# Cross-attention and mixture-of-experts block: a re-ordered prologue, with weight turns among the first row maxima and the first V projections inside batch 0

## The chip, the cores and the metric

The kernel runs on one core of one Trainium2 chip. The metric is the device time in microseconds (us); a figure for a kernel is the median of its runs. Engines are TensorE (PE, with its weight loads as PEld), VectorE (DVE), ScalarE (ACT), GpSimd (POOL) and SyncE (SP, which here only issues DMAs).

## The reference

For 8 batches of x with 256 rows and 512 columns. The attention works on the normalised rows of x as channels, the 512 columns being tokens; the feed-forward part works on rows as tokens of width 512.

```
t = layernorm(x)                       # over the 512 columns
q, k, v = Wq@t + bq, Wk@ctx + bk, Wv@ctx + bv          # 256x256 weights
dot = einsum('bhdt,bhds->bhts', q, k) / 4              # 16 heads of 16
mask = tmask[..., :, None] * smask[..., None, :]       # all ones here
dot = mask*dot - (1 - mask)*1e6
x = x + einsum('bhts,bhds->bhdt', softmax(dot)*mask, v)
n = layernorm(x)
x = x + n + shared_ffn(n) + top2_of_8_experts(n)       # 512 -> 352 -> 512
```

All is float32 but the experts, which are bfloat16.

## The kernel before

Order is by hand: each engine runs its instructions in the order in which the program issues them, and the framework adds only the waits that data and buffers need. A buffer pool with n buffers makes the (n+1)th tile of a tag wait for the readers of the first.

Prologue (lines 117 to 196 and 953 to 989). DMAs go out on two queues: SP carries x, ctx, the transposed-mask rows `mnat` and the bias of V `bvb`; ACT carries Wq, the broadcast mask `mb`, Wk, Wv and four small DMAs of the biases of q and k (L140). The biases are turned on TensorE (L145), and 16 small VectorE operations (L148 to L161) make the columns `alpha`, `beta`, `mine`, from which `extra_rows` makes, for each head group and side, a 128x512 tile that is added to q or k and holds bias and masking rows. Wq, Wk and Wv are turned on TensorE in `turn_square` and copied to SBUF by ScalarE. VectorE takes the statistics of x (L302 to L305), GpSimd the inverse square root (L307), VectorE normalises to `xm` (L326) and multiplies it by the mask (L328), GpSimd multiplies ctx by the mask (L314).

A head group G is half of the heads that one projection makes: `project_qk(G, side)` gives q or k for G and G + 1 with two accumulated matmuls, each recorded as two, into one bank (L373), and two VectorE operations out of it (L379). There are 4 groups to a batch, 32 in all.

The softmax of a group needs row maxima first: `row_max` multiplies q by k on 32-row tiles of the array (two logical matmuls, four recorded, L390) into a two-bank tile of `ps_s`, and VectorE reduces it (L392). Eight of these make a group; `take_max` turns the maxima and subtracts them from q (L398, L399). Then `exp_scores` multiplies the other way round (L410) and ScalarE takes exp (L412); `attend` multiplies by V (L425), four 32-column tiles each.

The first loop (L982, called the head loop here) makes the ten row maxima that run ahead: all eight of G = 0 and two of G = 1. They alternate between the banks `s1` and `s2`. After every second one of the first eight, `project_v` projects a quarter of V (psv, L342; VectorE, L346); the router's weights are turned after the first; `take_max(0)` follows the eighth.

The main loop runs over batches b, groups g and steps h = 0 to 7: a step is one row maximum for the next group and one exp, with attend in every second step, and projections, the division, the residual and other work in fixed steps. `plan` is a list of further thunks per step of a batch (step n = 8g + h). In batch 0 it holds eight `clear` DMAs that write zeros to DRAM and ten turns of the shared expert's weights (`weight_thunks`: 6 `up_rows` of four transposes, 4 `down_rows` of three; each call also issues loads, up to three ahead, on SP), whose copies `evacuate` deals out to VectorE and ScalarE in turn. `load_batch(b + 1)` is called in step 6.

Buffers that matter: `ps_m` tag `mm` has two banks for all turns, projections and V; `ps_s` has one tile for `s1` and one for `s2`; `acc` (five buffers) holds the natural weights and biases before they are turned; `extra` has three; `ctx` and `mb` one each.

Of the kernel before, what the change touches and what calls it, by code (L numbers as in the profile page):

```python
# [9 lines left out]
F32 = mybir.dt.float32  # L10
# [3 lines left out]
ALU = mybir.AluOpType  # L14
# [20 lines left out]
def xattn_ffn_kernel(  # L35
# [76 lines left out]
    def load_square(W):  # L112
        nat = five.tile([P, 2, C], F32, tag="acc", name="wnat")
        nc.scalar.dma_start(out=nat, in_=W.rearrange("(o p) c -> p o c", p=P))
        return nat

    wq_nat = load_square(Wq)
    load_batch(0, (nc.sync, nc.scalar))
    wk_nat, wv_nat = load_square(Wk), load_square(Wv)


# [9 lines left out]

    bnat = five.tile([2 * NG, 4, 2, HD], F32, tag="acc", name="bnat")
    nc.vector.memset(bnat, 0.0)
    for side, bias in enumerate((bq, bk)):
        by_group = bias.rearrange("(c a j d) -> a c j d", a=2, j=4, d=HD)
        for a in range(2):
            row = NG * side + 2 * a
            nc.scalar.dma_start(out=bnat[row : row + 2, :, a, :], in_=by_group[a])  # L140
    alpha = const.tile([P, 2, 2, NG // 2], F32, name="alpha")
    beta = const.tile([P, 2, 2], F32, name="beta")
    mine = const.tile([P, 2], F32, name="mine")
    pt = ps_m.tile([P, 2, 2, NG // 2], F32, tag="mm", name="pt")
    nc.tensor.transpose(  # L145
        pt.rearrange("p s a c -> p (s a c)"), bnat.rearrange("r j a d -> r (j a d)"), ident[: 2 * NG, : 2 * NG]
    )
    nc.vector.tensor_scalar(alpha[:, 0], pt[:, 0], 0.25, None, ALU.mult)  # L148
    nc.vector.tensor_copy(alpha[:, 1], pt[:, 1])
    for a in range(2):  # L150
        r = HD * (1 - a)
        R0, R1, R2 = (rowis[:, r + i : r + i + 1] for i in range(3))
        nc.vector.tensor_reduce(mine[:, a : a + 1], rowis[:, HD * a : HD * a + HD], AX.X, ALU.add)
        nc.vector.tensor_scalar(beta[:, 0, a : a + 1], R0, -BIG, None, ALU.mult)
        nc.vector.tensor_add(beta[:, 1, a : a + 1], R0, R1)
        for R, big in ((R1, -BIG), (R0, BIG)):
            nc.vector.scalar_tensor_tensor(
                alpha[:, 0, a], R.to_broadcast([P, 2]), big, alpha[:, 0, a], ALU.mult, ALU.add
            )
        nc.vector.tensor_sub(alpha[:, 1, a], alpha[:, 1, a], R1.to_broadcast([P, 2]))  # L160
        nc.vector.tensor_add(beta[:, 1, a : a + 1], beta[:, 1, a : a + 1], R2)  # L161
    mhalf = const.tile([P, 1], F32, name="mhalf")
    nc.gpsimd.memset(mhalf, -0.5)
    rank = const.tile([P, E], F32, name="rank")
# [36 lines left out]
    ys = dram.tile([NT * P, T], F32, name="ys")  # L201
    ACC = [[dram.tile([P, T], F32, name=f"accd{b}_{tt}") for tt in range(2)] for b in range(NB)]

    WqT = wts.tile([P, 2, 2, 4, 2, HD], F32, name="WqT")
    WkT = wts.tile([P, 2, 2, 4, 2, HD], F32, name="WkT")
    WvT = wts.tile([P, 2, C], F32, name="WvT")

    def turn_square(nat):  # L210
        pt = ps_m.tile([P, 2, 2, P], F32, tag="mm", name="pt")
# [11 lines left out]
    def load_router():  # L223
        nat = five.tile([E, T], F32, tag="acc", name="wnat")
        nc.sync.dma_start(out=nat, in_=router_w)
        pt = ps_m.tile([P, NKC, E], F32, tag="mm", name="pt")
        for kc in range(NKC):
            nc.tensor.transpose(pt[:, kc, :], nat[:, kc * P : (kc + 1) * P], ident[:E, :E])
        nc.vector.tensor_copy(sguT[:, 1, :, I:], pt)

    def weight_thunks():


        def up_rows(W, dst, ic):
            i0, n = ICH[ic]
            nat = five.tile([P, T], F32, tag="acc", name="wnat")
            nc.sync.dma_start(out=nat[:n, :], in_=W[i0 : i0 + n, :])

            def go():
                pt = ps_m.tile([P, NKC, P], F32, tag="mm", name="pt")  # L240
                for kc in range(NKC):
                    nc.tensor.transpose(pt[:, kc, :n], nat[:n, kc * P : (kc + 1) * P], ident[:n, :n])
                evacuate(dst[:, :, i0 : i0 + n], pt[:, :, :n])

            return go

        def down_rows(W, dst, hc):
            nat = five.tile([P, I], F32, tag="acc", name="wnat")
            nc.sync.dma_start(out=nat, in_=W[hc * P : (hc + 1) * P, :])

            def go():
                pt = ps_m.tile([P, 3, P], F32, tag="mm", name="pt")
                for ic, (i0, n) in enumerate(ICH):
                    nc.tensor.transpose(pt[:n, ic, :], nat[:, i0 : i0 + n], ident)
                cols = slice(hc * P, (hc + 1) * P)
                evacuate(dst[:, 0:2, cols], pt[:, 0:2, :])
                evacuate(dst[: ICH[2][1], 2, cols], pt[: ICH[2][1], 2, :])
# [50 lines left out]
        return mv, rs  # L308


    def mask_context(b):
        s = S[b]
        for i in range(2):
            nc.gpsimd.tensor_mul(s["ctx"][:, i, :], s["ctx"][:, i, :], s["mb"])  # L314

    def start_stats(b, i):
        s = S[b]
# [9 lines left out]
        for i in range(2):  # L327
            engine.tensor_mul(xm[:, i, :], xm[:, i, :], s["mb"])  # L328

    def project_v(b, only=None):  # L330

        if only in (None, 0):
# [6 lines left out]
        for sc in range(4) if only is None else [only]:  # L339
# [15 lines left out]
    def extra_rows(G, side, engine):  # L355

        b, g = divmod(G, NG)
        if True:
            for a in range(2):
                t = three.tile([P, T], F32, tag="extra", name=f"extra{side}_{G + a}")  # L360
                engine.tensor_scalar(  # L361
                    t, S[b]["mb"], alpha[:, side, a, g // 2 : g // 2 + 1], beta[:, side, a : a + 1],
                    ALU.mult, ALU.add,
                )
                EXTRA[G + a, side] = t

    def project_qk(G, side):

        b, g = divmod(G, NG)
        W, rhs = ((WqT, S[b]["xm"]), (WkT, S[b]["ctx"]))[side]  # L370
# [1 line left out]
        for kc in range(2):  # L372
# [4 lines left out]
        for a in range(2):  # L377
            t = four.tile([P, T], F32, tag="qk"[side], name=f"{'qk'[side]}{G + a}")
            nc.vector.scalar_tensor_tensor(  # L379
                t, ps, mine[:, a : a + 1], EXTRA.pop((G + a, side)), ALU.mult, ALU.add  # L380
            )
            QK.setdefault(G + a, []).append(t)

    def row_max(G, tci, half, tag="s1"):

# [566 lines left out]

    for i in range(2):
        start_stats(0, i)
    extra_rows(0, 0, nc.vector)
    for nat, dst, scale in ((wq_nat, WqT, 0.25), (wk_nat, WkT, 1.0)):
        pt = turn_square(nat)
        for kc in range(2):
            for a in range(2):
                by_row = pt[:, kc, :].rearrange("p (c a j d) -> p c a j d", c=2, a=2, j=4)[:, :, a]  # L960
# [2 lines left out]
                    nc.scalar.copy(at, by_row)  # L963
                else:
                    nc.scalar.mul(at, by_row, scale)
    nc.scalar.copy(WvT, turn_square(wv_nat))
    start_norm(0, nc.vector)
    mask_context(0)


    mnat = five.tile([B * 4, P], F32, tag="acc", name="mnat")
    nc.sync.dma_start(out=mnat, in_=mask.rearrange("b o (c p) -> (b o c) p", p=P))
    mcol = const.tile([P, B * 4], F32, name="mcol")
    pt = ps_m.tile([P, B * 4], F32, tag="mm", name="pt")
    nc.tensor.transpose(pt, mnat, ident[: B * 4, : B * 4])
    nc.vector.tensor_copy(mcol, pt)
    nc.sync.dma_start(out=bvb, in_=bv.partition_broadcast(P))

    project_qk(0, 0)
    extra_rows(0, 1, nc.vector)  # L980
    project_qk(0, 1)
    for r in range(8 + LEAD):  # L982
        row_max(r // 8, r % 8 // 2, r % 2, ("s1", "s2")[r % 2])
        if r % 2 == 1 and r < 8:
            project_v(0, r // 2)
        if r == 7:
            take_max(0)
        if r == 0:
            load_router()
    weights = weight_thunks()  # L990
    casts, turns = expert_weights()
    V_AT = [(2, 5), (2, 7), (3, 1), (3, 3)]
    KEPT = 6
# [14 lines left out]
    for b in range(B):  # L1008
        plan = later + [[] for _ in range(STEPS - len(later))]
        if b == 0:  # L1010
            spread(plan, [(1.0, lambda e=e: clear(e)) for e in range(E)], [(3 * e + 8, 1) for e in range(E)])
            spread(plan, weights, [(n, 1) for n in (7, 11, 13, 15, 16, 23, 24, 27, 29, 31)])
        if 1 <= b <= 4:
            for n in range(6):
                plan[5 * n + 1].append(casts.pop(0))
# [18 lines left out]
        for g in range(NG):  # L1034
            G = NG * b + g
            for h in range(8):
# [23 lines left out]
                    start_stats(b + 1, h - 2)  # L1060
                if g == 1 and h == 5 and b + 1 < B:
                    start_norm(b + 1, nc.gpsimd)
                if (g, h) in V_AT and b + 1 < B:
                    project_v(b + 1, V_AT.index((g, h)))
                if g % 2 == 1 and h == 7 and G + 3 < last:
# [73 lines left out]
```

## Time and profile before

| | us |
|---|---|
| median of 3 runs | 918.92 |
| lowest, highest | 918.4, 925.13 |
| the profiled execution, its own time | 920.46 |
| its span in the profile | 918.7 |
| mean granted clock of TensorE | 0.987 |

Busy time of the engines in the stages that the change touches, from the view that sums busy time by stretch (length, then engine busy times with the number of instructions, the granted clock, the share of DMA and GB/s):

```profile
core 0: us, PE busy (x) PEld busy (x) DVE busy (x) ACT busy (x) POOL busy (x), PEclk, DMA share, GB/s
0.00:26.95 26.95, 10.11 (x23) 5.16 (x23) 12.88 (x37) 3.43 (x10) 10.06 (x54) 1.00 0.31 103
26.95:42.04 15.09, 13.36 (x64) 6.08 (x64) 13.96 (x21) 0.00 (x0) 1.52 (x2) 1.00 0.01 2
42.04:69.75 27.71, 24.67 (x105) 7.30 (x105) 14.27 (x15) 8.18 (x8) 3.25 (x3) 0.75 0.42 144
69.75:132.23 62.48, 55.43 (x376) 19.99 (x376) 44.97 (x68) 28.70 (x34) 17.92 (x18) 1.00 0.66 219
132.23:918.70 786.47, 745.93 (x4461) 308.34 (x4461) 508.58 (x927) 313.08 (x404) 237.18 (x247) 0.99 0.31 80
```

The rows are: the prologue up to the first row maximum; the head loop; group 0 of batch 0; groups 1 to 3; everything after. How to read it: the engine with the most busy time in a stretch is a candidate for what bounds it, but only the chain of waits says whether it was waited for. Times in the text are from the start of the span. A matmul's end is modelled, so overlapping matmuls can be listed with the same times.

### The profile page before, as it was taken

What the parts mean: (1) busy time and instruction counts of PE and PEld (TensorE: products, weight loads), DVE (VectorE), ACT (ScalarE), POOL (GpSimd) and SP (SyncE); (2) the same over time, 40 slices, a digit from 0 to 9 for tenths busy, and PEclk for the clock granted to TensorE, in tenths of its full rate; (3) what the DMA queues carried; (4) which work ended last, traced back from release to release, by engine and by line L of the source; (5) the groups of instructions that cost most, each with busy time, mean ns of one, the idle gap of its engine ahead of it and who ended that gap; (6) DMA issues with size and microseconds to landing.
All of it is one profiled execution on the core that took longest, in us unless ns stands there. A gap on an engine that the chain in (4) does not pass through costs nothing.

```text
span 918.7 us, 13426 instructions
## 1 busy us (share of the span) xinstructions
PE 849.5 (92%) x5027; PEld 346.9 (38%) x5027; DVE 594.7 (65%) x1064; ACT 353.4 (38%) x456; POOL 269.9 (29%) x324
## 2 busy tenths in 40 slices
PE   3887989999999999999999999999999899999875
PEld 1322333333333333433343334333434344445653
DVE  4847767785777677767776777677665732224477
ACT  1024444443344344434443434343434235555111
POOL 3114303532354235413450435052401110000551
PEclk9979999999999999999999999999999999999999
DMA  3049523112641353226321600020000033444785
GB/s 121 1 159 357 184 70 90 32 28 55 130 85 34 65 133 66 46 53 149 50 55 28 151 1 24 12 70 1 24 12 12 36 95 115 125 127 132 232 271 184
DMA packets 93080, 83.03 MB, mean 90 GB/s; under 512 B 58224, under 2 KB 74000, under 8 KB 92632
## 3 DMA queue, kind: packets, MB, share of 16 engines
q1 hardware_dynamic: 85360, 57.26, 21.8%
q0 software_dynamic: 4352, 19.67, 9.2%
q10 hardware_dynamic: 3304, 5.25, 1.6%
q8 instruction: 41, 0.67, 0.3%
q14 instruction: 23, 0.19, 0.1%
HBM read 41.91 MB, written 44.04 MB: 94 GB/s over the span
## 4 chain that ended last, share of the span: by engine, by line
PE 65%; DVE 16%; issue 10%; DMA 4%; POOL 3%; ACT 0%; DVEq 0%; ACTq 0%; SPq 0%; POOLq 0%
PE s L390 21%; PE av L425 9%; DVE nm L392 8%; PE psy L855 5%; PE psq L373 4%; PE pu L792 3%; PE eu L717 3%; PE eg L717 3%; PE ey L738 3%; PE psv L342 2%; PE s L410 2%; PE pgu L792 2%; PE psk L373 2%; PE pg L792 2%; DVE q L379 2%
## 5 line engine op out<-in xcount | busy, mean ns | idle before, releaser
L412 ACT ACTIVATE e<-s 128x1024 f32<-128x1024 f32 x256 | 262.0, 1023 | 431.9 <-PE s L410 431.7
L392 DVE TENSOR_REDUCE nm<-s 128x2 f32<-128x1024 f32 x256 | 312.8, 1223 | 143.1 <-PE s L410 132.4
L390 PE MATMUL s<-k,q 32*128 32x512 f32 x1024 | 289.7, 647 | 22.9 <-DVE nm L392 20.2
L410 PE MATMUL s<-q,k 32*128 32x512 f32 x1024 | 292.6, 648 | 0.0
L425 PE MATMUL av<-e,V 128*32 128x512 f32 x1024 | 137.8, 611 | 0.0
L390 PEld LDWEIGHTS s<-k,q 32*128 32x128 f32 x1024 | 77.1, 184 | 132.1 <-DVE nm L392 108.1
L307 POOL TENSOR_TENSOR rs<-ve,mhalf 128x1 f32<-128x1 f32 x32 | 18.3, 571 | 320.1 <-DVE ve L305 320.1
L361 POOL TENSOR_SCALAR extra<-mb,alpha,beta 128x512 f32<-128x512 f32 x60 | 46.2, 774 | 196.3 <-DVE q L379 195.2
L410 PEld LDWEIGHTS s<-q,k 32*128 32x128 f32 x1024 | 77.6, 185 | 3.4 <-issue 1.0
L425 PEld LDWEIGHTS av<-e,V 128*32 128x32 f32 x1024 | 20.2, 108 | 98.0 <-issue 97.9
L723 DVE SCALAR_TENSOR_TENSOR hz<-eth,eu 128x352 bf16<-128x352 f32 x35 | 18.2, 521 | 55.6 <-PE eu L717 49.4
L855 PE MATMUL psy<-sdT,h 128*128 128x512 f32 (+1 forms) x96 | 49.4, 627 | 5.0 <-DVE acc L861 3.5
L603 POOL DMA_INDIRECT xs<-xnb,at x28 | 28.0, 1002 | 70.5 <-DMA xs<-xnb,at 38.1
L373 PE MATMUL psq<-xm,WqT 128*128 128x512 f32 x64 | 35.3, 678 | 5.7 <-DVE xm L328 5.7
L766 POOL DMA_INDIRECT yg<-ys,yi x28 | 27.9, 997 | 33.6 <-DMA back<-accd 15.0
L717 PEld LDWEIGHTS <-late_ctx 128*128 128x128 bf16 x280 | 25.9, 97 | 27.5 <-issue 7.3
L792 PE MATMUL pu<-xT,sguT 128*128 128x256 f32 x128 | 35.9, 400 | 0.0
L792 PE MATMUL pg<-xT,sguT 128*128 128x256 f32 x128 | 35.0, 401 | 0.2 <-ACT logT L820 0.2
L342 PE MATMUL psv<-WvT,ctx 128*128 128x256 f32 x128 | 34.8, 394 | 0.0
L379 DVE SCALAR_TENSOR_TENSOR q<-psq,mine,extra 128x512 f32<-128x512 f32 x32 | 22.6, 746 | 17.9 <-PE psq L373 17.9
L792 PE MATMUL pgu<-xT,sguT 128*104 128x256 f32 (+1 forms) x128 | 33.8, 392 | 0.0
L743 ACT COPY ey<-ey 128x512 f32<-128x512 f32 x35 | 20.5, 586 | 32.7 <-PE ey L738 31.5
(189 smaller groups left out, 970.8 us busy)
## 6 DMA issues: line engine op xcount, KB each, us to landing
xs<-blank SPq DMA_DIRECT2D x8, 1792.0 KB
ys<-ey SPq DMA_DIRECT2D x35, 256.0 KB
x<-in_x_dram SPq DMA_DIRECT2D x8, 512.0 KB
ctx<-in_ctx_dram SPq DMA_DIRECT2D x8, 512.0 KB
back<-accd SPq DMA_DIRECT2D x14, 256.0 KB
out_dram<-back ACTq DMA_DIRECT2D x14, 256.0 KB
accd<-acc SPq DMA_DIRECT2D x12, 256.0 KB
gu<-in_L_ffn_w_gate_dram POOLq DMA_DIRECT2D x8, 352.0 KB
```

The source lines that it names most:

```text
L342: nc.tensor.matmul(ps, ct[:, kc, sc * P : (sc + 1) * P], WvT[:, kc, :], start=(kc == 0), stop=(kc == 1))
L361: engine.tensor_scalar(t, S[b]["mb"], alpha[:, side, a, g // 2 : g // 2 + 1], beta[:, side, a : a + 1], ALU.mult, ALU.add,)
L373: nc.tensor.matmul(ps, W[:, kc, g // 2].rearrange("p j a d -> p (j a d)"), rhs[:, kc, :], start=(kc == 0), stop=(kc == 1),)
L379: nc.vector.scalar_tensor_tensor(t, ps, mine[:, a : a + 1], EXTRA.pop((G + a, side)), ALU.mult, ALU.add)
L390: nc.tensor.matmul(ps[:, jj, :], q[r, tci * P : (tci + 1) * P], k[r, :], start=True, stop=True)
L392: nc.vector.reduce_max(NM[G % 2][:, tci, c0 : c0 + 33 : 32], ps, axis=AX.X)
L410: nc.tensor.matmul(ps[:, jj, :], k[r, sc * P : (sc + 1) * P], q[r, :], start=True, stop=True)
L412: nc.scalar.activation(e, ps, AF.Exp)
L425: nc.tensor.matmul(AVT[G][32 * j : 32 * j + 32, :], V[:, sc, 2 * g + j // 2, j % 2 : j % 2 + 2, :].rearrange("p o d -> p (o d)"), et[j // ...
L717: nc.tensor.matmul(ps, xT[:, kc, :], guT[:, bass.ds(e, 1), m, kc, :].rearrange("p o i -> p (o i)"), start=(kc == 0), stop=(kc == NKC - 1),)
L792: lambda kc=kc: nc.tensor.matmul(ps, gu[:, m, kc, i0 : i0 + n], xT[:, kc, :], start=(kc == 0), stop=(kc == NKC - 1))
L855: nc.tensor.matmul(t[0], get()[:n, ic, tt * P : (tt + 1) * P], d[:n, ic, :], start=(ic == 0), stop=(ic == 2))
```

## The change

- x of batch 0 is loaded first on SP, in two halves; then the four bias DMAs, now on SP, then ctx. ACT's queue keeps Wq, mask, Wk, Wv.
- The row terms (the bias transpose and the small VectorE operations) become a function, called after Wk is turned and after `xm` is made.
- The mask of ctx for batch 0 moves from GpSimd to VectorE; the four extras of groups 0 and 1 move from VectorE to ScalarE, as an activation with per-partition scale and bias.
- Wk and Wv are turned in the banks `s1` and `s2` of the scores; Wq stays in `mm`.
- k's second VectorE operation is issued after the first row maximum. The copies of `mcol` and of the router's turn go to ScalarE, and so do all copies of the shared expert's turns.
- In the head loop a turn of the shared expert's weights follows row maxima 1 to 6, 8 and 9 (eight of the ten); V is no longer projected there. Batch 0's plan keeps two turns, in steps 11 and 13.
- V of batch 0 is projected in group 0 of batch 0, in steps 0, 2, 5 and 7.

```diff
+    for i in range(2):
+        nc.sync.dma_start(out=S[0]["x"][:, i, :], in_=x[0, i * P : (i + 1) * P, :])
     wq_nat = load_square(Wq)
-    load_batch(0, (nc.sync, nc.scalar))
-    wk_nat, wv_nat = load_square(Wk), load_square(Wv)
+    nc.scalar.dma_start(out=S[0]["mb"], in_=mask[0, 0].partition_broadcast(P))
     bnat = five.tile([2 * NG, 4, 2, HD], F32, tag="acc", name="bnat")
...
-            nc.scalar.dma_start(out=bnat[row : row + 2, :, a, :], in_=by_group[a])
+            nc.sync.dma_start(out=bnat[row : row + 2, :, a, :], in_=by_group[a])
+    nc.sync.dma_start(out=S[0]["ctx"], in_=src[0].rearrange("(h p) t -> p h t", p=P))
+    wk_nat, wv_nat = load_square(Wk), load_square(Wv)
...
-                evacuate(dst[:, :, i0 : i0 + n], pt[:, :, :n])
+                nc.scalar.copy(dst[:, :, i0 : i0 + n], pt[:, :, :n])
...
+                if engine is nc.scalar:
+                    nc.scalar.activation(t, S[b]["mb"], AF.Identity, bias=be, scale=at)
...
-        for a in range(2):
+        def rows(a):
             t = four.tile([P, T], F32, tag="qk"[side], name=f"{'qk'[side]}{G + a}")
...
+        rows(0)
+        if one_now:
+            return rows
+        rows(1)
...
-    extra_rows(0, 0, nc.vector)
...
-    nc.scalar.copy(WvT, turn_square(wv_nat))
+    square(wq_nat, WqT, 0.25, ps_m, "mm")
     start_norm(0, nc.vector)
-    mask_context(0)
+    square(wk_nat, WkT, 1.0, ps_s, "s1")
+    row_terms()
+    mask_context(0, nc.vector)
+    wv = turn_square(wv_nat, ps_s, "s2")
+    extra_rows(0, 0, nc.scalar)
+    nc.scalar.copy(WvT, wv)
+    extra_rows(0, 1, nc.scalar)
+    project_qk(0, 0)
+    k_rows = project_qk(0, 1, True)
...
     for r in range(8 + LEAD):
         row_max(r // 8, r % 8 // 2, r % 2, ("s1", "s2")[r % 2])
-        if r % 2 == 1 and r < 8:
-            project_v(0, r // 2)
+        if r == 0:
+            k_rows(1)
+            pt = ps_m.tile([P, B * 4], F32, tag="mm", name="pt")
+            nc.tensor.transpose(pt, mnat, ident[: B * 4, : B * 4])
+            nc.scalar.copy(mcol, pt)
+            load_router()
+        elif r != 7:
+            weights.pop(0)[1]()
         if r == 7:
             take_max(0)
-        if r == 0:
-            load_router()
...
-            spread(plan, weights, [(n, 1) for n in (7, 11, 13, 15, 16, 23, 24, 27, 29, 31)])
+            spread(plan, weights, [(11, 1), (13, 1)])
...
+                if b == 0 and g == 0 and h in (0, 2, 5, 7):
+                    project_v(0, (0, 2, 5, 7).index(h))
```

More of the change, by code (lines that the diff above doesn't have):

```diff
@@ L115, in load_square @@
         return nat
-    wq_nat = load_square(Wq)
-    load_batch(0, (nc.sync, nc.scalar))
-    wk_nat, wv_nat = load_square(Wk), load_square(Wv)
-    ident = const.tile([P, P], F32, name="ident")
-    make_identity(nc, ident)
-    rowis = const.tile([P, 32], F32, name="rowis")
-    nc.vector.tensor_reduce(rowis, ident.rearrange("p (j r) -> p r j", j=4), AX.X, ALU.add)
+    S[0] = {
+        "x": two.tile([P, 2, T], F32, tag="x", name="x0"),
+        "mb": one.tile([P, T], F32, tag="mb", name="mb0"),
+        "ctx": one.tile([P, 2, T], F32, tag="ctx", name="ctx0"),
+    }
+    for i in range(2):
+        nc.sync.dma_start(out=S[0]["x"][:, i, :], in_=x[0, i * P : (i + 1) * P, :])
+    wq_nat = load_square(Wq)
+    nc.scalar.dma_start(out=S[0]["mb"], in_=mask[0, 0].partition_broadcast(P))
     bnat = five.tile([2 * NG, 4, 2, HD], F32, tag="acc", name="bnat")
@@ L139, in xattn_ffn_kernel @@
             row = NG * side + 2 * a
-            nc.scalar.dma_start(out=bnat[row : row + 2, :, a, :], in_=by_group[a])
+            nc.sync.dma_start(out=bnat[row : row + 2, :, a, :], in_=by_group[a])
+    nc.sync.dma_start(out=S[0]["ctx"], in_=src[0].rearrange("(h p) t -> p h t", p=P))
+    wk_nat, wv_nat = load_square(Wk), load_square(Wv)
+    ident = const.tile([P, P], F32, name="ident")
+    make_identity(nc, ident)
+    rowis = const.tile([P, 32], F32, name="rowis")
+    nc.vector.tensor_reduce(rowis, ident.rearrange("p (j r) -> p r j", j=4), AX.X, ALU.add)
     alpha = const.tile([P, 2, 2, NG // 2], F32, name="alpha")
@@ L143, in xattn_ffn_kernel @@
     mine = const.tile([P, 2], F32, name="mine")
[L144 to L149, printed above, removed]
-    for a in range(2):
[L151 to L161, printed above, removed]
     mhalf = const.tile([P, 1], F32, name="mhalf")
@@ L202, in xattn_ffn_kernel, with row_terms @@
     ACC = [[dram.tile([P, T], F32, name=f"accd{b}_{tt}") for tt in range(2)] for b in range(NB)]
+    def row_terms():
+        pt = ps_m.tile([P, 2, 2, NG // 2], F32, tag="mm", name="pt")
+        nc.tensor.transpose(
+            pt.rearrange("p s a c -> p (s a c)"), bnat.rearrange("r j a d -> r (j a d)"), ident[: 2 * NG, : 2 * NG]
+        )
+        nc.vector.tensor_scalar(alpha[:, 0], pt[:, 0], 0.25, None, ALU.mult)
+        nc.vector.tensor_copy(alpha[:, 1], pt[:, 1])
+        for a in range(2):
+            r = HD * (1 - a)
+            R0, R1, R2 = (rowis[:, r + i : r + i + 1] for i in range(3))
+            nc.vector.tensor_reduce(mine[:, a : a + 1], rowis[:, HD * a : HD * a + HD], AX.X, ALU.add)
+            nc.vector.tensor_scalar(beta[:, 0, a : a + 1], R0, -BIG, None, ALU.mult)
+            nc.vector.tensor_add(beta[:, 1, a : a + 1], R0, R1)
+            for R, big in ((R1, -BIG), (R0, BIG)):
+                nc.vector.scalar_tensor_tensor(
+                    alpha[:, 0, a], R.to_broadcast([P, 2]), big, alpha[:, 0, a], ALU.mult, ALU.add
+                )
+            nc.vector.tensor_sub(alpha[:, 1, a], alpha[:, 1, a], R1.to_broadcast([P, 2]))
+            nc.vector.tensor_add(beta[:, 1, a : a + 1], beta[:, 1, a : a + 1], R2)
     WqT = wts.tile([P, 2, 2, 4, 2, HD], F32, name="WqT")
@@ L208, in xattn_ffn_kernel, with turn_square @@
     WvT = wts.tile([P, 2, C], F32, name="WvT")
-    def turn_square(nat):
-        pt = ps_m.tile([P, 2, 2, P], F32, tag="mm", name="pt")
+    def turn_square(nat, pool, tag):
+        pt = pool.tile([P, 2, 2, P], F32, tag=tag, name="pt")
         for kc in range(2):
@@ L228, in load_router @@
             nc.tensor.transpose(pt[:, kc, :], nat[:, kc * P : (kc + 1) * P], ident[:E, :E])
-        nc.vector.tensor_copy(sguT[:, 1, :, I:], pt)
+        nc.scalar.copy(sguT[:, 1, :, I:], pt)
     def weight_thunks():
@@ L255, in go @@
                 cols = slice(hc * P, (hc + 1) * P)
-                evacuate(dst[:, 0:2, cols], pt[:, 0:2, :])
-                evacuate(dst[: ICH[2][1], 2, cols], pt[: ICH[2][1], 2, :])
+                nc.scalar.copy(dst[:, 0:2, cols], pt[:, 0:2, :])
+                nc.scalar.copy(dst[: ICH[2][1], 2, cols], pt[: ICH[2][1], 2, :])
             return go
@@ L308, in norm_stats, with mask_context @@
         return mv, rs
-    def mask_context(b):
+    def mask_context(b, engine=nc.gpsimd):
         s = S[b]
         for i in range(2):
-            nc.gpsimd.tensor_mul(s["ctx"][:, i, :], s["ctx"][:, i, :], s["mb"])
+            engine.tensor_mul(s["ctx"][:, i, :], s["ctx"][:, i, :], s["mb"])
     def start_stats(b, i):
@@ L328, in start_norm, with project_v @@
             engine.tensor_mul(xm[:, i, :], xm[:, i, :], s["mb"])
-    def project_v(b, only=None):
-        if only in (None, 0):
+    def project_v(b, only):
+        if only == 0:
             V = two.tile([P, 4, HEADS // 2, 3, HD], F32, tag="V", name=f"V{b}")
@@ L338, in project_v @@
         by_pair = lambda t: t.rearrange("p (h o d) -> p o h d", o=2, d=HD)
-        for sc in range(4) if only is None else [only]:
+        for sc in (only,):
             ps = ps_m.tile([P, C], F32, tag="mm", name="psv")
@@ L360, in extra_rows, with project_qk @@
                 t = three.tile([P, T], F32, tag="extra", name=f"extra{side}_{G + a}")
[L361 to L364, printed above, removed]
+                at, be = alpha[:, side, a, g // 2 : g // 2 + 1], beta[:, side, a : a + 1]
+                if engine is nc.scalar:
+                    nc.scalar.activation(t, S[b]["mb"], AF.Identity, bias=be, scale=at)
+                else:
+                    engine.tensor_scalar(t, S[b]["mb"], at, be, ALU.mult, ALU.add)
                 EXTRA[G + a, side] = t
-    def project_qk(G, side):
+    def project_qk(G, side, one_now=False):
         b, g = divmod(G, NG)
@@ L376, in project_qk @@
             )
-        for a in range(2):
+        def rows(a):
             t = four.tile([P, T], F32, tag="qk"[side], name=f"{'qk'[side]}{G + a}")
@@ L954, in xattn_ffn_kernel, with square @@
         start_stats(0, i)
-    extra_rows(0, 0, nc.vector)
-    for nat, dst, scale in ((wq_nat, WqT, 0.25), (wk_nat, WkT, 1.0)):
-        pt = turn_square(nat)
+    def square(nat, dst, scale, *where):
+        pt = turn_square(nat, *where)
         for kc in range(2):
@@ L973, in xattn_ffn_kernel @@
     mcol = const.tile([P, B * 4], F32, name="mcol")
-    pt = ps_m.tile([P, B * 4], F32, tag="mm", name="pt")
-    nc.tensor.transpose(pt, mnat, ident[: B * 4, : B * 4])
-    nc.vector.tensor_copy(mcol, pt)
     nc.sync.dma_start(out=bvb, in_=bv.partition_broadcast(P))
-    project_qk(0, 0)
-    extra_rows(0, 1, nc.vector)
-    project_qk(0, 1)
+    weights = weight_thunks()
     for r in range(8 + LEAD):
         row_max(r // 8, r % 8 // 2, r % 2, ("s1", "s2")[r % 2])
-        if r % 2 == 1 and r < 8:
-            project_v(0, r // 2)
+        if r == 0:
[6 more added lines that the diff above has]
+            weights.pop(0)[1]()
         if r == 7:
             take_max(0)
-        if r == 0:
-            load_router()
-    weights = weight_thunks()
     casts, turns = expert_weights()
```

## The prediction

> **What bounds the kernel now.** I read the page's chain that ended last, then the same chain in order of time for the first 50 us, then the matmul timeline for how far apart the steps of the head loop lie, then the busy time and granted clock in stretches of 3.41 us. The change touches only the prologue and batch 0, so these are the views that matter. The chain in order of time:
> ```profile
> 1.24 6.80 DMA ctx<-in_ctx_dram
> 8.06 2.00 DMA bnat<-in_L_xattn_bk_dram
> ...
> 14.96 3.79 DVE xm L326 x2
> ...
> 19.49 3.75 PE psq L373 x4
> 23.24 2.87 PE psk L373 x4
> 26.14 0.76 DVE k L379
> 26.95 1.13 PE s L390 x4
> ```
> Until 10 us everything waits for the last bias, whose DMA was issued only when ctx had landed; its transpose stands first in TensorE's queue. Then VectorE carries the chain. The two normalisations take 3.79 us, and two rows of the sources by line say why that is odd:
> ```profile
> L326 DVE TENSOR_SCALAR xm<-x,mv,rs x2: 1555/1978/2400, 14.9 to 16.3; 128x512 f32<-128x512 f32 x2
> L486 DVE TENSOR_SCALAR xn<-acc,mv,rs x1: 540/540/540, 841.6 to 841.6; 128x512 f32<-128x512 f32 x1
> ```
> The same form takes 0.54 us late in the kernel. The slow pair lies beside GpSimd's mask of ctx (L314, 14.89 to 17.55).
>
> The clock, in stretches that end where the granted clock changes:
> ```profile
> 39.06:42.48 3.42, 1.83 (x11) 0.75 (x13) 3.04 (x6) 0.00 (x0) 0.00 (x0) 1.00 0.02 5
> 42.48:45.89 3.41, 3.41 (x10) 1.01 (x8) 1.86 (x2) 0.59 (x1) 0.00 (x0) 0.50 0.00 0
> 45.89:49.30 3.41, 3.41 (x9) 1.00 (x6) 1.23 (x1) 1.23 (x2) 0.00 (x0) 0.50 0.00 0
> 49.30:52.72 3.42, 3.42 (x8) 1.19 (x10) 0.44 (x1) 0.22 (x1) 0.00 (x0) 0.50 0.00 0
> ...
> 59.54:62.96 3.42, 1.60 (x16) 0.31 (x8) 2.19 (x2) 1.66 (x2) 1.36 (x2) 1.00 0.89 304
> 62.96:66.37 3.41, 3.28 (x16) 0.71 (x16) 1.23 (x2) 1.02 (x1) 1.12 (x1) 0.50 1.08 383
> 66.37:69.78 3.41, 2.69 (x24) 1.19 (x20) 2.07 (x4) 1.02 (x1) 0.00 (x0) 1.00 1.09 386
> ```
> A stretch with little array work (39.06, 59.54) is followed by half clock, and two stretches in which TensorE was busy throughout (42.48, 45.89) did not bring the clock back, because 32-row matmuls fill a quarter of the array each. Before 42 us the view prints 1.00 for want of a record; the projections there take 0.85 us a matmul against 0.48 later, so the clock was half until about 25.4 us.
>
> **What the Trainium skill says.** (1) "TensorE: Matmul & The Clock Gate", Part 1: the clock is halved or full, decided per free-running window of about 3.4 us by how busy the array was. The trace agrees: 0.50 or 1.00, held for 3.41 us or multiples. (2) The same page, Part 4: a transpose on TensorE "doesn't count as PE-busy the same way". Half agrees: the stretch from 66.37, eight transposes among its 24, kept its clock with otherwise less work than the one from 59.54, so they count for something. (3) "SBUF — State Buffer", "SBUF: two separate sides": VectorE in a two-port mode and GpSimd lock each other out of a shared port pair. 2.40 and 1.56 us against 0.54 agree.
>
> **A measure of array work.** One unit is a 32-row matmul of 512 columns, or a 128-column transpose, a quarter of 0.48 us. A full projection matmul is 4 units, one of V 2, one of the attend's (32 columns) 1. Counted from the timeline: clock lost after 39.06 (10 units) and 59.54 (11); held after 25.41 (12.5); not regained after 18.58 (10.4) or 45.89 (9.8); regained after 49.30 (15) and 62.96 (14). So a window needs somewhere between 11 and 12.5 units to hold, 10.4 to 14 to recover.
>
> **The change part by part.**
>
> Front. x now has SP's queue to itself ahead of the biases and ctx; ACT's queue loses the four bias DMAs and carries Wq, mask, Wk, Wv. Wq landed at 5.7 us (the fourth SP DMA, bvb, was released by it then); I take x's second half at 5.5 (bounds 4.5 and 8.0, the latter ctx's landing). VectorE no longer waits for the biases: statistics 0.61 + 0.18 + 0.15 plus gaps, 6.5; GpSimd's power 0.57, 7.1; xm 0.54, 7.65; two mask products 1.27, 8.95. TensorE: Wq's turn from 5.7 (12 turns took 3.11, so 1.04 for four), Wk's, then the bias transpose. The last bias waits for Wq or x at worst (5.7), plus 2.0 of flight: 7.8 (bounds 5 and 10). Wv's turn ends about 9.2, psq starts at 9.3. The 14 small row-term operations (10.58 to 11.95, 1.4 us), then the ctx mask on VectorE (2 x 0.67), run from 8.95 to 11.7 beside psq; ctx sits behind six DMAs and lands at about 9.3. All are done before psk at 12.7, so they cost nothing; if ctx came after 11.4, psk would slip. The four extras move to ACT, idle until 45.3 us: nearest row, its 128x512 copy, 0.58 each (bounds 0.5 to 1.0), hidden by psq. Wk and Wv in the scores' banks remove the 0.33 and 0.42 us waits for a bank, counted in the turns. psq and psk took 6.62; with the clock coming back anywhere in a window I take 6.1, so psk ends 15.4, k's first STT 0.76, first row maxima T = 16.2 (bounds 14.5 and 18.5). Before: 26.95. **-10.75.**
>
> Head loop. Before, it ran from 26.95 to 42.04, 15.1 us, VectorE-bound (10 x 1.23 plus V's 4 x 0.6), with two row maxima often overlapping on different rows of the array. Now a turn stands between each two, so none overlap, and TensorE is the bound: 1.08 + 0.59 = 1.67 us a step at full clock (V's STTs gone, VectorE needs 1.23). One wait is new: k's second STT is queued on VectorE behind the first row maximum, and the router's transposes need psk's bank, which that STT frees; the second row maximum stands behind them. TensorE has 1.07 us of work, then waits until T + 3.1, and restarts at T + 3.5. If those transposes got the other bank this would be 1.4 us less (the low bound); nothing in the trace settles it, and I take the wait. At full clock: six steps with turns (two of them smaller) about 10, the eighth with its maximum and take_max 2.6, two more with turns of three 3.2: 19.3 us.
>
> At half clock a row maximum takes 1.69 (42.04) and a turn about 0.95 (0.75 the smaller ones): 3.5 + 6 x 2.65 + 3.2 + 2 x 2.45 = 27.5 us.
>
> Which? Around T, from psk's end to T + 3.5, lie 4.3 us with 4 units in them; a window of 3.41 starting anywhere from 1.7 before T to 2.6 after it holds under 11, and that is longer than a window. The clock is lost. Then the loop at half clock gives 8 units per 2.65 us, 10.3 a window, even if transposes count in full: not regained. **+12.4.**
>
> V in batch 0. h = 0, 5, 7 had about 1.3 us of slack on TensorE (2.45 a step with 1.12 of scores): free, as the steps of the next batch with V at 2.46 show. h = 2 also attends: 1.12 + 1.0 + 1.06 = 3.3, +0.5. Starting at half clock h0 takes 4.1 and h1 3.9; V and psq bring the clock back (full-array work), then 3.3 + 2.98 + 2.77 + 2.46 + 2.65 + 2.46: 24.6. Before: 42.04 to 69.75, 27.7, part of it at half clock (h1 took 7.04, h6 4.20). **-3.1.**
>
> Turns out of the steps: of ten, eight leave. The steps that held them took 2.45 to 2.46, the same as empty ones; only 0.19 (2.65, with attend) and about 0.1 more is saved. **-0.3.** Their copies leave VectorE, where they hid behind TensorE: 0.
>
> Queues: SP issues ten weight loads some 45 us earlier, into an idle time of DMA, ahead of x for batch 1; that x is needed near 77 us. ctx for batch 1 waits for the fourth V instead of psk, some 7 us; GpSimd masks it for psk at 99 us. The eight clears follow without the turns between them. GpSimd loses 2.66 us early. All 0.
>
> Sum -10.75 + 12.4 - 3.1 - 0.3 = **-1.75** against the profiled span of 918.7 (the execution 920.46). The median shown is 918.92, so 917.
>
> **Rivals.**
> A (0.62), above: the gain of the front is eaten by a head loop at half clock. 917; own range 913 to 920.5.
> B (0.28): the clock holds or returns within one or two windows, because weight loads or transposes count for more than I have it. For: full-clock steps give 8 units per 1.67 us, 16 a window, enough once regained. Against: the gap at T. Held throughout: 16.2 + 19.3 = 35.5, G0 at full clock 22.05, -12.2 - 0.3: 906.4. One or two windows lost cost 1.3 to 2.6 us: 908 to 909.
> C (0.10), slower: the turns taken out of batch 0 were the filler that kept the clock in steps without attend. Each lost window costs what h6 showed, 4.20 - 2.65 = 1.55. Two lost windows turn A into a loss; four give 923. Against: from 142 to 170 us, steps without filler kept 1.00.
> D: x in halves does nothing by itself. In before x was long there (statistics began at 11.95 without a wait); the early start comes from the order of work. If the biases again land at 10, T moves by 2 us: 919. Inside A's range.
>
> **Numbers.** 917 is A. The range 906.5 to 920.5 leaves out part of C and slow A, and the edge of B. One per cent is 9.2 us, about what a measurement tells from no change: faster than 909.7 has most of B, 0.23; slower than 928.1 needs seven lost windows or more, 0.03; within 0.74.
>
> **What would show it.** First row maxima near 16 us; L326 near 0.54; a clock of 0.50 in the stretches from about 19 to 45; row maxima of the head loop 2.6 us apart; first exp near 45. If they lie 1.7 us apart at 1.00, A is wrong and B right. If psq starts after 11, the front is wrong. If batch 0's later steps show new stretches at 0.50, C.

## The result and the profile after

| | before | after |
|---|---|---|
| median of 18 runs each, us | 918.62 | 911.88 |
| lowest, highest | 917.36, 925.13 | 908.25, 918.96 |
| the profiled execution, its own time | 920.46 | 909.48 |
| mean granted clock in it | 0.987 | 0.989 |

The ratio is 0.9922, 95% interval [0.9902, 0.9942]: 0.8% faster, about 6.7 us. The predicted 917 is 5 us too slow; its range held the time. The two profiled executions differ by more, 11.0 us: that of before lies 1.8 us above its median, that of after 2.4 us below its own. The runs of the new kernel spread over 11 us: 15 of the 18 lie between 908 and 914, three between 915 and 919. The last experiments come back to that spread.

Busy time by stretch of the kernel after, with the columns of the table shown for before. The stretches are again the prologue, the head loop, group 0, groups 1 to 3 and the rest:

```profile
0.00:14.72 14.72, 7.80 (x21) 4.26 (x21) 9.62 (x33) 6.36 (x14) 6.46 (x51) 1.00 0.63 203
14.72:34.38 19.66, 18.51 (x80) 7.41 (x80) 13.01 (x12) 4.21 (x10) 2.00 (x3) 0.84 0.33 101
34.38:58.59 24.21, 22.67 (x118) 8.65 (x117) 15.41 (x21) 8.72 (x10) 0.77 (x1) 0.92 0.05 12
58.59:120.43 61.84, 52.24 (x351) 17.35 (x351) 42.73 (x63) 27.35 (x32) 20.42 (x20) 1.00 0.74 247
120.43:907.70 787.27, 746.22 (x4461) 308.37 (x4461) 509.03 (x926) 313.02 (x403) 238.59 (x247) 0.99 0.32 79
```

Against before, by lengths: prologue -12.23, head loop +4.57, group 0 -3.50, groups 1 to 3 -0.64, rest +0.80, together -11.0. In the head loop TensorE is now busy for 18.5 of 19.7 us where it had been busy for 13.4 of 15.1: it took the bound over from VectorE, as its loop of one maximum and one turn implies; its last two steps ran at half clock, which the experiments take up.

The chain of waits of after, in order of time, through the prologue and into the loop (start, length, what):

```profile
1.73 5.32 DMA wnat<-in_L_xattn_Wk_dram
7.09 1.11 PE pt L225 x4
...
9.45 2.64 PE psq L385 x4
12.09 1.73 PE psk L385 x4
13.92 0.76 DVE k L392
14.72 1.13 PE s L408 x4
```

No wait for x, for the biases or for the normalisation stands on it any more. The chain waits for the DMA of Wk, then runs on TensorE. The normalisation, which had carried it for 3.79 us, takes 0.54 and 0.72 us beside it (L337 now, in the timeline).

### The profile page after: what moved, and what is told of

Read it like the earlier page. It is cut to its first block, busy times and chain, and to the rows that moved or that the text cites. A ratio compares the mean times of both kernels' runs of the same rounds, so it can differ in the third digit from the quotient of the medians.

```text
span 907.7 us, 13439 instructions
## 1 busy us (share of the span) xinstructions
PE 847.4 (93%) x5027; PEld 346.0 (38%) x5027; DVE 589.8 (65%) x1053; ACT 359.7 (40%) x469; POOL 268.2 (30%) x322
## 4 chain that ended last, share of the span: by engine, by line
PE 66%; DVE 15%; issue 9%; DMA 5%; POOL 4%; ACT 1%; ACTq 0%; DVEq 0%; SPq 0%; POOLq 0%
PE s L408 22%; PE av L443 9%; DVE nm L410 8%; PE psy L873 4%; PE psq L385 3%; PE pu L810 3%; PE eu L735 3%; PE eg L735 3%; PE ey L756 3%; PE psv L353 2%; PE s L428 2%; PE pgu L810 2%; PE pg L810 2%; PE psk L385 2%; DMA back<-accd 2%
## 5 line engine op out<-in xcount | busy, mean ns | idle before, releaser
L385 PE MATMUL psq<-xm,WqT 128*128 128x512 f32 x64 | 32.6, 633 | 0.0
L735 PE MATMUL eg<-guT,late_ctx 128*128 x140 | 29.8, 311 | 2.7 <-DMA late_ctx<-xs 2.6
```

The costliest lines, as they stand in the source:

```text
L385: nc.tensor.matmul(ps, W[:, kc, g // 2].rearrange("p j a d -> p (j a d)"), rhs[:, kc, :], start=(kc == 0), stop=(kc == 1),)
L735: nc.tensor.matmul(ps, xT[:, kc, :], guT[:, bass.ds(e, 1), m, kc, :].rearrange("p o i -> p (o i)"), start=(kc == 0), stop=(kc == NKC - 1),)
```

## The experiments

The theory after the result: the gain is the front's; the loop and V cancel; and the loop kept its clock because the wait that I had taken at its start did not arise. Rivals: that the new loop itself brings something, or that the clock has another cause.

**The front alone.** The head loop, V and turns of before, behind the new front:

```
-        elif r != 7:
-            weights.pop(0)[1]()
+        if r % 2 == 1 and r < 8:
+            project_v(0, r // 2)
...
-            spread(plan, weights, [(11, 1), (13, 1)])
+            spread(plan, weights, [(n, 1) for n in (7, 11, 13, 15, 16, 23, 24, 27, 29, 31)])
...
-                if b == 0 and g == 0 and h in (0, 2, 5, 7):
-                    project_v(0, (0, 2, 5, 7).index(h))
```

> The changed front with the head loop, the V projections and the weight turns where they were before. Theory 1 (the new head loop gives back about as much as the later steps gain, +4.6 against -3.5 and -0.6 in the profile after): the first row maxima start near 14.7 us and the time is about that of the whole change, 907 to 912 us. Theory 2 (the parts taken out of group 0 and out of the plan are worth more than the head loop costs): 914 us or more. A head loop of 15 us at full clock is expected in both.

Measured: 910.24 (906.98 to 911.81), ratio 0.9881 [0.9855, 0.9908]. First row maximum at 14.84. Its loop takes 15.58 us and its group 0 28.08, together 43.66; in the change 19.66 + 24.21 = 43.87. The front is worth the whole gain; loop and V exchange 4 us between two stages. The ratio of the front alone is even a little below that of the whole change (0.9922 [0.9902, 0.9942]), with intervals that only just overlap: loop and V add nothing to the time, and may cost some.

**The loop alone.** The loop, V, two turns in the plan and ScalarE's copies, behind the front of before:

```
-        if r % 2 == 1 and r < 8:
-            project_v(0, r // 2)
-        if r == 7:
-            take_max(0)
         if r == 0:
             load_router()
-    weights = weight_thunks()
+        elif r != 7:
+            weights.pop(0)[1]()
+        if r == 7:
+            take_max(0)
...
+                if b == 0 and g == 0 and h in (0, 2, 5, 7):
+                    project_v(0, (0, 2, 5, 7).index(h))
```

> The front of before with the new head loop, V in group 0 and the turns' copies on ScalarE. Theory 1: within 2 us of before, 916.5 to 920.5. Theory 2: faster than before by 4 us or more. If the clock is lost at the start of the loop in most runs, as was predicted, 919 us or more with row maxima 2.6 us apart.

Measured: 919.23 (914.54 to 923.94), ratio 0.9989 [0.9971, 1.0007]: nothing. Its prologue showed something else. Busy time by stretch, in three successive stretches of 3.41 us (PE busy is the first engine; the granted clock is third from the end):

```profile
10.34:13.76 3.42, 3.40 (x14) 2.56 (x14) 3.01 (x21) 1.71 (x9) 0.57 (x1) 1.00 0.31 91
13.76:17.17 3.41, 0.05 (x1) 0.00 (x0) 3.38 (x6) 0.43 (x1) 3.04 (x3) 1.00 0.62 202
17.17:20.59 3.42, 2.01 (x3) 1.01 (x4) 1.96 (x4) 0.00 (x0) 1.12 (x2) 0.50 0.00 0
```

The first holds twelve turns of 128 columns and two small ones, no other matmul; they ran at half speed (3.11 us for twelve, against 0.59 for four in the loop). The records of the clock begin at 13.76, at 1.00 (the 1.00 printed before is for want of a record), and the next, empty, stretch is followed by 0.50. So turns alone brought the clock back: they count. How much is worked out in the next section.

**Turns after pairs.** A turn only after every second row maximum, so that two maxima can overlap on different rows of the array:

```
-        elif r != 7:
+        elif r % 2 == 1:
             weights.pop(0)[1]()
...
-            spread(plan, weights, [(11, 1), (13, 1)])
+            spread(plan, weights, [(n, 1) for n in (11, 13, 15, 27, 29)])
```

> The whole change, but turns only after every second row maximum (five of them), the other five back in steps of batch 0 that have room. Theory 1 (TensorE bounds the head loop at 1.65 us a step because a turn stands between every two row maxima; VectorE needs 1.23): the loop takes 13 to 15 us in place of 19.7, the time is 904 to 907 us. Rival (the single turns are what keeps the clock, 8 units per 1.65 us): the clock is lost in the loop, which then takes 20 us or more, and the time is 911 us or more.

Measured: 903.27 (902.23 to 904.01), ratio 0.9809 [0.9786, 0.9833]. Busy time by stretch (prologue, head loop, group 0):

```profile
0.00:14.78 14.78, 7.76 (x22) 4.18 (x22) 9.62 (x33) 6.36 (x14) 6.47 (x51) 1.00 0.65 202
14.78:29.42 14.64, 13.15 (x69) 5.37 (x69) 12.06 (x12) 3.20 (x7) 2.01 (x3) 1.00 0.33 99
29.42:54.13 24.71, 23.15 (x116) 8.45 (x117) 15.99 (x21) 8.19 (x8) 0.77 (x1) 0.93 0.05 11
```

The loop is 5.0 us shorter than the change's, at the granted clock of 1.00, and group 0 takes 0.5 more. Two things are in the 5.0 us. TensorE's timeline of after shows two row maxima at full clock and the last two of the loop:

```profile
22.66 1.13 PE L408 MATMUL s<-k,q 32*128 32x512 f32 x4
24.30 1.13 PE L408 MATMUL s<-k,q 32*128 32x512 f32 x4
...
28.70 2.07 PE L408 MATMUL s<-k,q 32*128 32x512 f32 x4
31.54 2.08 PE L408 MATMUL s<-k,q 32*128 32x512 f32 x4
```

The last two steps take 2.84 us each at half clock (28.70 to 34.38) instead of about 1.65, so 2.4 of the 5.0 us are clock that the loop with pairs kept. The other 2.6 us go with the turns: where TensorE is the bound, they cost their length.

**A turn into the gap at take_max.** In the change the clock falls in the stretch that holds take_max's wait for the eighth maximum. Busy time by stretch of after:

```profile
21.42:24.83 3.41, 3.41 (x18) 1.44 (x16) 2.68 (x3) 1.19 (x3) 0.00 (x0) 1.00 0.37 107
24.83:28.25 3.42, 2.61 (x15) 0.97 (x11) 2.68 (x3) 0.64 (x2) 0.00 (x0) 1.00 0.63 206
28.25:31.66 3.41, 3.37 (x10) 1.29 (x10) 1.53 (x2) 0.02 (x1) 0.00 (x0) 0.50 0.02 5
```

PE busy falls from 3.41 to 2.61 us in the middle one, and the clock is at 0.50 behind it. The timeline of TensorE in the same place (start, length; in brackets the idle time and its releaser) has the reason, the last part of take_max waiting for the reduction:

```profile
25.84 1.13 PE L408 MATMUL s<-k,q 32*128 32x512 f32 x4
26.90 0.55 PE L416 MATMUL psn<-ident,nm 128*128 128x128 f32 x3
28.30 0.48 PE L416 MATMUL psn<-ident,nm 128*128 128x128 f32 x1 [0.85 <-DVE nm L410]
```

The turn of the seventh maximum was moved behind the eighth (`r != 7` becomes `r != 6`).

> The whole change with the turn after the seventh row maximum moved behind the eighth, into TensorE's wait for the last maximum (0.85 us in the profile after). Theory (that wait is what loses the clock at 28 us and makes the last three row maxima 2.84 us apart): the clock is held to the end of the loop in most runs, which gives 3 to 4 us: 907 to 909 us. Rival (the clock is lost by where the window falls, whatever the wait): gain of the wait alone, 0.5 us or less.

Measured: 909.0 (903.72 to 913.59), ratio 0.9859 [0.982, 0.9897]. Mixed: three of six runs lie at 903.7 to 907.3, with a mean granted clock of 0.995 or 0.996, and three at 910.8 to 913.6, with 0.979 to 0.990. The profiled one, among the latter, lost its clock all the same at 30.31; 0.84 us of that wait were left. Two of the runs that kept their clock (904.0 and 903.7) are as fast as the kernel with pairs, and they still have single turns between the row maxima. So a good part of what the kernel with pairs gains over the change is the clock that it keeps, and not the length of the turns. Where those runs kept their clock is not shown, since none of them was profiled.

**The predicted wait, put in.** In the change the router's turn starts without it. TensorE's timeline of after:

```profile
16.17 0.22 PE L239 MATMUL pt<-ident,wnat 8*128 8x8 f32 x1 [0.30 <-ACT mcol L1009]
```

VectorE's timeline of after:

```profile
17.04 0.74 DVE L392 SCALAR_TENSOR_TENSOR k<-psk,mine,extra 128x512 f32<-128x512 f32 x1
```

It took the bank of `mcol`, freed by ScalarE's copy, 0.9 us before k's second operation began to read the other. The experiment turns the router's weights in the scores' bank `s1` instead, which the first reduction has to free:

```
-        pt = ps_m.tile([P, NKC, E], F32, tag="mm", name="pt")
+        pt = ps_s.tile([P, NKC, E], F32, tag="s1", name="pt")
```

> The whole change, but the router's transposes use the bank of the first row maximum, so that they and the second row maximum behind them wait for VectorE's first maximum (about 1.3 us more of idle TensorE at the start of the head loop, much like the wait that the prediction assumed). Theory (less array work in the window there than holds the clock, and a loop at half clock does not get it back): the clock is 0.50 through the loop in most runs, row maxima 2.5 to 2.7 us apart, 915 to 920 us. Rival (the loop's own work brings the clock back within two windows, or the clock holds): 1.3 to 3 us over the whole change, 913 to 915 us.

Measured: 919.89 (917.28 to 923.4), ratio 1.0021 [1.0006, 1.0037], all 15 runs at a mean clock of 0.975 to 0.980. The timeline of TensorE in this kernel:

```profile
17.68 0.22 PE L239 MATMUL pt<-ident,wnat 8*128 8x8 f32 x1 [1.31 <-DVE nm L410]
```

And its busy time by stretch:

```profile
15.75:19.17 3.42, 2.11 (x17) 0.87 (x13) 2.18 (x3) 0.37 (x2) 1.52 (x3) 1.00 0.23 81
19.17:22.58 3.41, 3.41 (x13) 1.30 (x11) 1.94 (x2) 0.58 (x1) 0.00 (x0) 0.50 0.42 130
22.58:25.99 3.41, 3.41 (x10) 1.53 (x12) 1.44 (x2) 1.06 (x2) 0.00 (x0) 0.50 0.19 53
```

One wait of 1.3 us cost the clock for nine stretches (19.17 to 49.89): steps of 2.84 to 3.06 us instead of 1.53 to 1.65, a loop of 28.54 us (15.23 to 43.77) instead of 19.66, and 8 us of the time. That is the prediction's likeliest case, reproduced: it put 27.5 us and 917.

**Parts of the front**, on the kernel with turns after pairs. First, the mask of ctx back on GpSimd (`mask_context(0)`):

> Turns after pairs, with the first batch's ctx masked on GpSimd again. Theory 1 (in the new order ctx lands after the normalisation, so GpSimd no longer meets it): L337 stays at 0.54 to 0.75 us, first row maximum within 0.4 us of 14.8, time within 1 us of the run of turns after pairs. Theory 2 (the move off GpSimd is what shortened the normalisation): L337 at 1.5 to 2.4 us again, first row maximum near 17, 905 us or more.

Measured: 905.46 (904.18 to 910.19). The normalisation was not slowed (0.54 and 0.55 us): with the new order of loads GpSimd waited for ctx until 10.57, long after it. The 2.40 us of before were a collision of time, which the later ctx alone resolves. The first row maximum comes at 16.07, 1.3 us later than in the first profile of pairs, but the chain of waits puts none of that on the mask: Wk landed at 7.67 instead of 7.09, q's projection took 3.32 us instead of 2.54, and k's followed it at once at 13.43, when GpSimd's mask (10.57 to 13.07) was done. Three of its four runs lie within what pairs took in all its runs (902.2 to 907.9, below), the fourth at 910.2.

Second, the four bias DMAs on ACT's queue behind Wk and Wv:

> Turns after pairs, with the four bias DMAs on ACT's queue behind Wk and Wv, as before; all else as there. Theory 1 (the biases' landing still gates the front through their transpose, which stands before Wv's turn and psq): landing at 9 to 10 us, psq at 10.3 to 11.3 in place of 9.24, first row maximum 1 to 2 us later, 904.5 to 905.5 us. Theory 2 (with the row terms behind the normalisation the biases have slack): no change, 903 to 904 us.

Measured: 906.61 (904.73 to 910.71). First row maximum at 18.04; in the chain of waits:

```profile
1.73 7.63 DMA wnat<-in_L_xattn_Wk_dram
9.39 1.59 DMA bnat<-in_L_xattn_bk_dram
...
11.11 0.24 PE pt L200
11.35 1.04 PE pt L228 x4
12.40 3.02 PE psq L388 x4
```

The bias transpose waits for its last DMA until 11.11, and Wv's turn and q stand behind it: the first row maximum is 3.3 us later than in the first profile of pairs (14.78). The biases' own wait is the smaller part of that. With their four DMAs gone from SP, ctx was issued at 1.65 us instead of 6.34, and Wk landed at 9.37 instead of 7.09: that is 2.3 of the 2.8 us by which q's projection began later, and the bias transpose then held TensorE for 0.59 us more. So by the profile the order of the loads is a real part of the front; late biases and an early ctx came in one edit, and that ctx slowed Wk's load is likely, not shown. The time alone doesn't show it, since its median lies within what pairs took. The other parts of the front (the row terms behind the normalisation, the extras on ScalarE, the banks of the scores for the turns) were not taken out singly.

Third, k's second operation at once, and a second turn after the tenth maximum:

```
-    k_rows = project_qk(0, 1, True)
+    project_qk(0, 1)
...
-            k_rows(1)
...
-            weights.pop(0)[1]()
+            for _ in range(2 if r == 9 else 1):
+                weights.pop(0)[1]()
...
-            spread(plan, weights, [(n, 1) for n in (11, 13, 15, 27, 29)])
+            spread(plan, weights, [(n, 1) for n in (11, 13, 15, 27)])
```

> Turns after pairs, with k's second operation issued at once (VectorE is idle while the first row maximum is multiplied) and a second turn after the tenth row maximum, into TensorE's 0.73 us wait there. Theory: 0.7 us less in the head loop, which VectorE bounds, and 4 more units of array work ahead of group 0, so that the clock holds in more runs: 901 to 902.5 us. Rival: the deferral of k costs nothing, 903 to 904 us.

Measured: 903.71 (901.45 to 904.93), ratio 0.9844 [0.9827, 0.986]. Its profiled execution kept its clock through batch 0; its time does not set it apart from the other kernel with pairs.

**x in one load**, twice, and the two other kernels once more beside it:

```
-    for i in range(2):
-        nc.sync.dma_start(out=S[0]["x"][:, i, :], in_=x[0, i * P : (i + 1) * P, :])
+    nc.sync.dma_start(out=S[0]["x"], in_=x[0].rearrange("(h p) t -> p h t", p=P))
```

The first time:

> The kernel with turns after pairs, but x of batch 0 comes in one DMA of 512 KB instead of two of 256 KB; nothing else changes. Theory 1: the halves pay only as far as the statistics of the first half (which began at 3.6 us) run ahead of the second half's landing (5.2 us). With one load both wait for about 5.2, the second half's square root comes at about 7.3 instead of 6.9, the mask product ends at about 9.6 instead of 9.15, and q is projected some 0.5 us later: first row maxima at 15.3 instead of 14.8, time 903 to 905. Theory 2 (the prediction's rival D for the halves): Wk's turn, the bias transpose and ScalarE's copies of the turned Wk and Wq are as late as xm, so the halves are worth nothing: first row maxima at 14.8 within 0.15, time 902 to 904. Against both: one large DMA lands earlier than two, or delays Wq behind it, by which T moves by more than 0.8 us.

Then pairs, x in one load and the change, all on one chip:

> The kernel with turns after pairs once more, as the one that the next two are measured against on the same chip. 902 to 904.5; first row maxima at 14.5 to 16.2, by where the clock's 3.41 us windows fall: the theory is that the window phase is free from run to run, so that the projection of q takes anything from 2.0 (full clock) to 3.5 us (half clock) at the same start of 9.4 to 9.7 us.

> The same with x of batch 0 in one load, once more. Theory 1: only the window phase made the last such run's first row maxima 1.0 us later (q's projection began at 9.60 in both); then over more runs the two kernels agree within 0.5 us. Theory 2: Wq's turn and the statistics 1.1 us later leave less array work in the window before the projection of q, so that the clock comes back a window later in most runs; then this kernel stays 1 to 2.5 us behind the other.

> The change itself on the same chip: 908 to 914 with single runs to 919, so 5 to 10 us behind the kernel with turns after pairs. If it lies within 3 us of that kernel here, the chips and not the turns made the difference between the earlier calls.

Measured: x in one load 905.21 (904.82 to 908.62), then 904.76 (903.23 to 908.58); beside the latter pairs again 906.71 (902.18 to 907.87), ratio 0.9842 [0.9814, 0.987] against 0.9844 [0.9818, 0.9871]; the change again 912.16 (910.15 to 919.72), ratio 0.9935 [0.9904, 0.9967]. In halves or not, q's projection began at 9.37 to 9.60. The halves are worth nothing that can be told; the 1.0 us in the first pair of profiles was the length of q's projection, 3.57 against 2.54 us. Pairs stay 5 us ahead of the change on one chip.

The repeat of pairs, with nothing changed, has its own lesson. Busy time by stretch:

```profile
13.75:17.16 3.41, 2.32 (x14) 0.86 (x15) 2.18 (x3) 0.37 (x2) 1.71 (x3) 1.00 0.14 24
17.16:20.57 3.41, 3.41 (x12) 1.57 (x12) 1.96 (x3) 0.59 (x1) 0.77 (x1) 0.50 0.52 187
20.57:23.99 3.42, 3.42 (x14) 1.72 (x12) 2.00 (x3) 0.59 (x1) 0.00 (x0) 0.50 0.26 68
```

Its first row maximum is at 14.54, and a stretch happened to begin 0.79 us ahead of it. That stretch held the gap before the row maxima and the two after the first, the clock was lost at 17.16 and stayed at half until 41.1. In the first profile of the same program a stretch began only 0.24 us ahead (14.54, with the row maximum at 14.78), held enough, and the loop ran at full clock. The executions took 907.87 and 902.52 us, on two chips; on the chip of the repeat alone, the six runs go from 902.18 us at a mean clock of 0.996 to 907.87 at 0.982. So in these two profiles the phase of the stretches, which the program does not set, decided. The change's runs at 915 to 919 (five of 26 in all) have a mean granted clock of 0.977 to 0.979, the other 21 of 0.983 to 0.990, and the kernel with the wait put in has 0.975 to 0.980 in every run. So those five lost about as much clock as that kernel does. That they lost it in the same place is likely, not shown: none of them was profiled.

## Why the prediction was right or wrong

**Front, -10.75: right, -12.23 in the profile.** The mechanism is as worked out: VectorE 0.54 and 0.72 us for the two halves where 0.54 each was put, all of its work beside Wk's turn and q, psq from about 9.3 (the row terms are 16 operations, not 14, in the time that was put for them). That this start came out is in part luck: Wq landed at 4.4 us, not 5.7, and TensorE then waited for Wk's own load until 7.1, a wait that was not priced. The sum was too slow by 1.5 us at its end: q and k took 4.4 us, not 6.1, because the clock came back inside q's projection. The repeat of the change, where it came back later, has 15.58 and -11.4. ScalarE's extras took 0.76 to 0.81 us, not 0.58, hidden as said; a plain copy was the wrong row for them. The Trainium skill's "ScalarE: Activation LUTs", section "What ACT_TABLE_LOAD costs", has 186 ns for an activation, 93 more for each per-partition operand and 0.833 ns for each element, an estimate of 0.80 us for 512 elements and two such operands, with which the trace agrees. The Trainium skill's "SBUF — State Buffer", section "SBUF: two separate sides", had been cited for the slow normalisation; the experiment with the mask on GpSimd agrees: with no overlap, 0.54 and 0.55 us.

**Head loop, +12.4: wrong, +4.57.** The failed step is "nothing in the trace settles it, and I take the wait": router behind k's second operation, restart at T + 3.5. The restart came at T + 1.45, from the other bank. So the conclusion "The clock is lost." at T fell in the profiled run, and the loop ran at 1.65 us a step, which is the prediction's own figure for full clock (1.67), until take_max's wait. From there it ran at half clock for three stretches, 2.84 us a step. The prediction named no loss of the clock at take_max. This is rival B with three stretches lost; the prediction gave 908 to 909 for one or two, and the profiled execution took 909.48. With the wait put in, the failed case comes out as worked out (28.5 for 27.5 us). So the mechanism of that case, a wait that loses the clock and a loop that cannot win it back, and its size are borne out; which bank the turn got was a coin that I called wrongly, and gave 0.62 of the chance.

**The measure of array work: held.** It had 11 to 12.5 units as the bound. In after a full-array matmul of psk takes 1.73 / 4 = 0.43 us, so a full stretch holds 32 units, and that bound is 0.34 to 0.39 of it. Counted the same way over the experiments, as a share of what a full array would do: clock lost at 0.37 (the change, 24.83), 0.36 (pairs, 28.20) and 0.29 (the wait, 15.75); held at 0.39 (pairs, 14.54) and 0.40 (the change, 14.59); regained at 0.38 (the transposes alone: twelve times a quarter of 0.43 us in 3.41) and 0.41 (the change, 35.07), not at 0.23 to 0.38 (the wait, and the repeat of pairs). In all fourteen profiles, up to 690 us, no stretch above 0.37 lost the clock and none below 0.39 held it. One bound, near 0.38, fits both ways. These shares are estimates from counts of matmuls and their lengths, good to 0.01 or 0.02, so the bound is known no better than that. One reading of the prediction needs a correction: the records of the clock in the profile of before begin at 25.41, not at 42; its conclusion, half clock until about 25.4, stands.

**The skill on transposes.** "TensorE: Matmul & The Clock Gate", Part 4, was taken as half true, with transposes still counted as a unit each. The loop-only kernel decides for the counting: a stretch of nothing but transposes brought the clock back, at 0.38 when each counts as a unit. So for these float32 transposes, which the traces record as matmuls against the identity, the sentence does not hold; whether they run in the mode that the page means, the traces do not say. Part 1 agrees in every profile: the clock is halved or full by stretches of 3.41 us, and these run free, so that their phase varies between runs of one kernel.

**V in batch 0, -3.1: right, -3.50** (24.21 against 24.6). **Turns out of the steps, -0.3: -0.64** for groups 1 to 3, no larger than can vary. The rest, put at nothing, took 0.80 more in the profile.

**Rival C**, filler missing later in batch 0, did not occur: after 38.49 the next half clock is at 721 us. **Rival D**: the first half of it holds (x in halves does nothing by itself), and its fear of late biases is in part borne out, 3.3 us of the front for late biases and an early ctx together, but in the change they were in time.

**The sum** of -1.75 is -11.0 in this profile and -6.7 in the medians. The likeliest case was the wrong one, and the range reached to the right one because the unsettled bank had kept both ends. That the range held the time owes more to its width than to the case that it was built on.

## What to carry to other kernels

Where small-tile matmuls keep a clock only just, count the array work of each stretch of 3.41 us, transposes included, around every wait that a change adds or moves; a wait of 1.3 us cost 8 us here. Put filler where another engine is the bound and the array would idle, not between matmuls that could overlap: with turns after pairs the kernel took 5 us less than the change on one chip (906.71 and 912.16), part of it turns and part of it clock. When two banks are equally possible for a tile, say so and price both, since one may decide the sign of a term.

## What the runs showed of the hardware that was not expected

- Lost at half clock: a loop that does 1.53 to 1.65 us a step at full clock and 2.84 to 3.06 at half stayed at half clock for nine stretches, in eight of them with TensorE busy for all of the 3.41 us, until projections on the full array came (about 0.45 of full work in the last of the nine, then a clock of 1.00).
- What a phase is worth: by where the 3.41 us stretches fall, q's projection took 2.28 to 3.57 us at almost the same start (9.37 to 9.60), and two profiled executions of one program lie 5.4 us apart.
- The second normalisation of x takes 0.72 us in the change, beside GpSimd's clear of `blank` (7.25 to 7.76), and 0.55 with the mask on GpSimd, where that clear comes after it. In the kernel with the front alone two clears lie beside it, of V and of `blank` (7.18 to 8.16), and it takes 1.18. So a plain memset on GpSimd also slows VectorE here, by 0.17 us for one and 0.63 for two.
